# Cross-attention and a LoRA mixture-of-experts layer on one core: the read-outs and scores of a quad gathered in one place

## The chip, the core and the metric

The kernel runs on one core of a Trainium2 chip. The metric is the device time of one launch in microseconds (us); the median of three runs of the kernel before is 1106.21 us (1106.09 to 1106.55). The engines are named as the profile names them: PE (TensorE matmul), PEld (TensorE weight load), DVE (VectorE), ACT (ScalarE), POOL (GpSimd) and SP (SyncE, which issues all DMAs here).

## The reference

The input x has 8 batches of 1024 rows of 1024 numbers; each batch has 64 memory rows and a mask over them. Everything is float32.

```python
h = layernorm(x)                                     # no weights
attn = softmax(where(mask, h @ memory.T / 32, -1e30))
x = x + where(any(mask), attn @ memory, 0)           # attention over 64 memory rows
h = layernorm(x)
base = h @ weight.T                                  # 1024 x 1024
probs = softmax(h @ router_w.T)                      # 8 experts
w = top-2 of probs, normalised, as a dense [rows, 8]
low = h @ lora_A.T                                   # 8 experts x rank 16 = 128 columns
out = x + base + 2 * ((low weighted by w) @ lora_B)
```

## The kernel before

**Tiles.** The 8192 rows are 64 tiles of 128 rows. Two tiles are a *pair* (0 to 31), four pairs are one batch, and two pairs are a *quad*. `quad(u)` works for u = 2, 4, ..., 30; the pairs 0 and 1 are done in `first()`. Inside a quad, u and v = u+1 are the pairs whose feed-forward part is computed. The pairs n = u+2 and m = u+3 have their attention finished in the same quad, and f = u+4 (and in the changed kernel g = u+5) have theirs begun. A quad is *far* while f exists (u up to 26).

**Order.** All five engine queues are written by hand (`tc.manual_schedule`): the order of the calls in `quad` is the order of each engine's instructions, and every engine works through its own queue in that order. What an instruction waits for is set by the tiles that it reads, and by the buffers that it takes over.

**Feed-forward.** The product h @ weight.T of a pair is done by a Strassen-Winograd scheme of seven block products. Product 1 is done for each pair alone (`product(u, 1)`, tile `ch`, 4 matmuls of 128x512); `product(u, 8)` adds the low-rank part to the same bank. Products 6, 2, 7, 3, 5 and 4 are done for both pairs of the quad by a second Strassen level (`joint(i, u, hooks)`, banks `jl` and `ju`, matmuls of 128x256, steps p4, chain, p2, p5, chain, p5, chain). `hooks[k]` are calls that are set between the steps. The sums of operands are POOL's (`rt_sums`, `rt_sum_3`, `joint_sums`, `six_add`), the additions of results into x are DVE's.

**Low rank and router.** `rt_turn_tile` turns the normalised rows (DVE transposes into hA and hB), `rt_low_rank_tile` multiplies them with 136 columns (tile `pa`), ACT copies the result (`axl`), `rt_top` makes the two weights on DVE, and `rt_turn_low_rank` turns it for the low-rank product (PE `trw`, ACT `axwt`).

**Attention of a pair.** `att_turn` turns x (DVE, `xs` into `xT`, two transposes of 128x1024). `att_scores` makes the scores with 16 matmuls of 64 columns, the two tiles in two halves of the array (`sct`). `att_sc` turns them back (`sc`), `att_rstd`, `att_shift`, `att_exp` and `att_divide` are the softmax on DVE and ACT, `att_turn_p` turns the weights (`ptp`, copied by ACT to `pt`). `att_readout` multiplies them with the memory in 4 matmuls of 64 rows and 512 columns into 4 banks (`ro`), and `att_add` adds the banks to x on DVE. The row statistics of x are ACT's (`x_sums`, `x_squares`, `x_root` for attention, `f_sums`, `f_squares`, `f_std` for the feed-forward, `f_rows` for the normalised rows, which go to DRAM and back as `hs`).

**What shares room.** One PSUM bank serves `sct`, `sc` and `ptp` in turn (`ps_at`), one serves `pa` and `trw` (`ps_rt`), and six serve all the rest (`ps_pp`: `ch` of both pairs, `ro`, `jl`, `ju`). A pool called `ring` has five tiles of 4 KB a partition, for `xs`, `xT`, `h`, `hs` and the blocked memory `ms`.

**The stretch that the change is about** runs from product 1 of u to the start of joint product 6 (the *head* of the quad). Before, PE does there, for u from 4 to 26: product 1 of u, `pa` of u, read-out of n, scores of m, `trw` of u, product 1 of v, product 8 of u, `pa` of v, read-out of m, scores of f. Every second quad (u = 4, 8, ..., 24) f begins a new batch, and then the memory of that batch is turned and centred in the head too (`load_ms`, `turn_mem`, `centre_turned` with the matmul `means`).

Of the kernel before, what the change touches and what calls it, by code (L numbers as in the profile page):

```python
# [10 lines left out]
F32 = mybir.dt.float32  # L11
# [13 lines left out]
def kernel(  # L25
# [61 lines left out]
    def transpose_blocked(dst, src):  # L87

        nc.vector.transpose(  # L89
            dst.rearrange("p k (t i) -> p t k i", i=NB),  # L90
            src.rearrange("p t (k i) -> p t k i", i=NB),
        )

    xts, xss, mems = {}, {}, {}

    def load_xs(u: int):

        xss[u] = []
        for r in range(2):
            xs = ring.tile([P, 4, QD], F32, tag="ring", name=f"xs_{u}_{r}")  # L100
            load_blocked(xs, xf[(2 * u + r) * P : (2 * u + r + 1) * P, :])
            xss[u].append(xs)

    def load_xt(u: int):
        xts[u] = []
# [237 lines left out]
    def load_ms(b: int):  # L343

        msr = ring.tile([P, D], F32, tag="ring", name=f"ms_{b}")
        n = M // NB * QD
        ms = msr[:, :n].rearrange("p (t c) -> p t c", c=QD)
        load_blocked(ms, mem[b])
        ones = msr[:, n : n + P]
        nc.gpsimd.memset(ones, 1.0 / D)  # L350
        mcs[b] = ms, ones, msr[:, n + P : n + P + M], msr

    def turn_mem(b: int):

        mt = memp.tile([P, KD, M], F32, tag="memT", name=f"memT_{b}_True", bufs=1)
        ms, ones, of_k, msr = mcs[b]
        transpose_blocked(mt, ms)
        if b == 1:
            nc.vector.tensor_reduce(of_k, mt.rearrange("p k m -> p m k"), AX.X, ALU.add)
        else:  # L360
            by = nc.gpsimd.tensor_tensor
            s4 = msr[:, : 4 * M].rearrange("p (k m) -> p k m", m=M)
            by(s4, mt[:, :4], mt[:, 4:], ALU.add)
            by(s4[:, :2], s4[:, :2], s4[:, 2:], ALU.add)
            by(of_k, s4[:, 0], s4[:, 1], ALU.add)
        mem_ts[b, True] = mt

    def centre_turned(b: int):

        _, ones, of_k, _ = mcs.pop(b)  # L370
        mt = mem_ts[b, True]
        means = bank_of(f"means_{b}")[:, :M]
        mm(means, ones, of_k, start=True, stop=True)
        tt(mt, mt, means.unsqueeze(1).to_broadcast([P, KD, M]), ALU.subtract)
# [16 lines left out]
    def xT_tile(u: int, r: int):  # L391
        t = ring.tile([P, KD, P], F32, tag="ring", name=f"xT_{u}_{r}")
        x_ts.setdefault(u, []).append(t)
        return t

    def att_turn_pe(u: int, r: int, later: bool = False):
        t = xT_tile(u, r)
        return transpose_pe((t[:, :KH, :], t[:, KH:, :]), xts[u][r], f"x{u}_{r}", later)

    def att_turn(u: int):  # L400
        for r in range(2):
            transpose_blocked(xT_tile(u, r), xss[u][r])

    def att_scores(u: int):

        mt = mem_ts[u // PPB, u > 1]
        sct = ps_at.tile([2 * M, P], F32, tag="at", name=f"sct_{u}")
        for k in range(KD):
            for r in range(2):
                mm(  # L410
                    sct[r * M : (r + 1) * M, :], mt[:, k, :], x_ts[u][r][:, k, :],
                    start=(k == 0), stop=(k == KD - 1),
                )
        scs[u] = small.tile([2 * M, P], F32, tag="tp", name=f"scts_{u}", bufs=2)
        nc.scalar.copy(scs[u], sct)
# [39 lines left out]
        tt(s, s, rden.unsqueeze(2).to_broadcast([P, 2, M]), ALU.mult)  # L455
        ps[u] = s

    def att_turn_p(u: int):
        ptp = ps_at.tile([2 * M, P], F32, tag="at", name=f"ptp_{u}")
        nc.tensor.transpose(ptp, ps.pop(u).rearrange("p j m -> p (j m)"), ident)  # L460
        pts[u] = small.tile([2 * M, P], F32, tag="tp", name=f"pt_{u}", bufs=2)
        nc.scalar.copy(pts[u], ptp)

    def att_readout(u: int):
# [13 lines left out]
    def att_add(u: int):  # L478
        for r in range(2):
            att_add_tile(u, r)  # L480
# [124 lines left out]
    def rt_turn_low_rank(u: int):  # L605
        axl = axls.pop(u)
        trw = ps_rt.tile([ER, 2, P], F32, tag="rt", name=f"trw_{u}")
        for r in range(2):
            nc.tensor.transpose(trw[:, r, :], axl[:, r, :ER], ident)  # L609
        axwts[u] = small.tile([ER, 2, P], F32, tag="axwt", name=f"axwt_{u}", bufs=2)  # L610
        nc.scalar.copy(axwts[u], trw)
# [66 lines left out]
    def add(u: int, bank, r: int, c: int):  # L678
        xc = xts[u][r][:, ts(c, HB)]
        tt(xc, bank, xc, ALU.add)  # L680
# [42 lines left out]
    def one_add(u: int):  # L723

        for to in ((0, 0), (0, 1), (1, 0)):
            add(u, pps[u][1], *to)

    def t_of(u: int):

# [43 lines left out]
        by(s3, up[:, :HK], lo[:, :HK], ALU.subtract)  # L773
        jss[i] = s1, s2, s3, s4

    def joint(i: int, u: int, hooks, final: bool = False):

# [15 lines left out]
        def to_x(p, src, first: int, n: int):  # L793
            if i == 6:
                t = t_of(p)[:, first : first + n]
                if n == HH and (p == u and first == 0 or v == NP - 1):
# [282 lines left out]

    def quad(u: int):  # L1080

        v, n, m, f = [u + i for i in range(1, 5)]
        more = n < NP
        far = f < NP
        b = f // PPB
        new_mem = far and f % PPB == 0

        product(u, 1, (lambda: att_sc(n)) if u == 2 else None, 1)
        if more and u > 2:
            x_sums(m)  # L1090
        if new_mem:
            mask_bias(b)
        pending.pop()()
        if u == 2:
            att_divide(n)
        one_add(u)
        rt_low_rank_tile(u, 0)
        if u == 2:
            att_turn_p(n)
        rt_low_rank_tile(u, 1)  # L1100
        if u == 2:
            att_turn(m)
        rt_turn_tile(v, 0)
        rt_top(u)
        rt_turn_tile(v, 1)
        rt_sum_3(u)
        rt_sums(v)
        if more and u > 2:
            x_squares(m)
        if new_mem:  # L1110
            load_ms(b)
        if far:
            load_xs(f)
            load_xt(f)
        if more:
            att_readout(n)
            att_scores(m)
            if u > 2:
                rt_turn_low_rank(u)
                x_root(m)  # L1120
                att_add(n)

        low_u = {3: lambda: rt_turn_low_rank(u)}
        if more:
            low_u = {0: lambda: att_sc(m), 2: lambda: product(u, 8)}
            if u == 2:
                low_u[1] = lambda: rt_turn_low_rank(u)
        product(v, 1, low_u)
        if more:
            att_rstd(m)  # L1130
            att_exp(m)
            if u == 2:
                att_add(n)
                att_divide(m)
        else:
            product(u, 8)
        product_add(u, 8)
        if more:
            f_sums(n)
            if u > 2:  # L1140
                att_divide(m)
        if new_mem:
            turn_mem(b)
        one_add(v)
        rt_low_rank_tile(v, 0)
        if more:
            att_turn_p(m)
        rt_low_rank_tile(v, 1, (lambda: centre_turned(b)) if new_mem else None)
        joint_sums(6, u)
        rt_sum_3(v)  # L1150
        if far:
            att_turn(f)
        rt_top(v)
        if more:
            f_squares(n)
            f_std(n)
            att_readout(m)
        if far:
            att_scores(f)
        if new_mem:  # L1160
            load_mem(b)
        if more:
            att_add(m)

        hooks = {7: [lambda: rt_turn_low_rank(v)]}
        if more:
            row_0, row_1 = f_rows_steps(n)
            hooks = {2: [row_0], 5: [lambda: rt_turn_low_rank(v), row_1]}
        end_6 = joint(6, u, hooks)
        joint_sums(2, u)  # L1170

        def low_v():
# [5 lines left out]
            for p in (u, v):  # L1178
                six_add(p)

        hooks = {1: [six]}
        if far:
            x_stats(f)
            hooks[3] = [lambda: att_sc(f)]
        if new_mem:
            void_mem(b)
        if (f + 2) % PPB == 0 and f + 2 < NP:
# [19 lines left out]
            hooks[5].append(lambda: att_exp(f))  # L1207
        end_3 = joint(3, u, hooks)
        joint_sums(5, u)
        if m + 2 < NP:  # L1210
            load_xs(m + 2)

        hooks = {1: [end_3]}
        if far:
# [8 lines left out]
        def rows_0():  # L1223
            end_5()
            for p in (u, v):
                store(p, 0)
                if not more:
                    store(p, 1, ts(1, HB))
            if m + 2 < NP:
                load_xt(m + 2)  # L1230

        hooks = {1: [rows_0]}
        if more:
            hooks[3] = [lambda: rt_sums(n)]
        if m + 2 < NP:
            hooks[5] = [lambda: att_turn(m + 2)]
        end_4 = joint(4, u, hooks, not more)

        def last():
# [56 lines left out]
```

## Time and profile before

| what | value |
|---|---|
| median of 3 runs | 1106.21 us (1106.09 to 1106.55) |
| the profiled execution, its time | 1106.56 us |
| its span, first to last instruction | 1104.7 us |
| PE busy | 1095.7 us (99%) |
| DVE busy | 810.8 us (73%) |
| POOL busy | 575.9 us (52%) |
| ACT busy | 555.3 us (50%) |
| granted TensorE clock | 1.000 |
| HBM traffic | 172.85 MB, 156 GB/s over the span |

A float32 matmul is two records in the trace, so that 16 matmuls are shown as x32. Matmuls overlap: how long one really takes is the distance from its start to the next one's start, not the length of its record. All times in the text are distances of starts where a row is followed by another on the same engine.

### The profile page before, as it was taken

How to read it: one execution, taken by the hardware profiler on the slowest of the kernel's cores; microseconds unless marked ns; L12 is line 12 of the kernel's file. 1: busy time of each engine (PE TensorE's matmuls, PEld its weight loads, DVE VectorE, ACT ScalarE, POOL GpSimd, SP SyncE). 2: the span in 40 equal slices, each digit the busy share in tenths (PEclk: the TensorE clock that was granted, in tenths of full speed). 3: DMA queues.
4: the chain of work that ended last, by engine and by line, in shares of the span. 5: the costliest groups of instructions: out<-in, count | busy, mean ns of one | idle time of the engine just before them, and what ended most of it. 6: DMA issues, size and time to landing. Idle time of an engine off the chain costs nothing.

```text
span 1104.7 us, 17542 instructions
## 1 busy us (share of the span) xinstructions
PE 1095.7 (99%) x5864; PEld 848.1 (77%) x5864; DVE 810.8 (73%) x2063; ACT 555.3 (50%) x1063; POOL 575.9 (52%) x647
## 2 busy tenths in 40 slices
PE   8999999999999999999999999999999999999998
PEld 6554787887878778787887878778787887878877
DVE  6666968777786768867678686777868787686665
ACT  4577554718357282663727547173562826545010
POOL 0079564735637265473635647266372744637382
PEclk9999999999999999999999999999999999999999
DMA  9857356374554735456265553754446453532301
GB/s 230 210 177 222 113 166 201 100 238 132 154 182 136 222 109 183 151 164 218 77 211 162 154 190 101 215 166 157 153 139 203 145 190 132 158 131 91 138 1 77
DMA packets 104922, 174.01 MB, mean 158 GB/s; under 512 B 12929, under 2 KB 77441, under 8 KB 104833
## 3 DMA queue, kind: packets, MB, share of 16 engines
q1 hardware_dynamic: 104832, 172.90, 50.3%
q8 instruction: 47, 0.77, 0.3%
q14 instruction: 43, 0.34, 0.1%
HBM read 107.84 MB, written 65.01 MB: 156 GB/s over the span
## 4 chain that ended last, share of the span: by engine, by line
PE 98%; DVE 1%; ACT 0%; DMA 0%; issue 0%; SPq 0%; DVEq 0%; ACTq 0%
PE jl L691 28%; PE ju L691 21%; PE pa L569 11%; PE ch L691 10%; PE sct L410 6%; PE ro L471 5%; PE ju L683 4%; PE jl L683 3%; PE plain L691 3%; PE ch L683 2%; PE j L691 1%; PE trw L609 1%; DMA xt<-in_x_dram 0%; PE tr_x L385 0%; PE b L691 0%; PE ptp L460 0%
## 5 line engine op out<-in xcount | busy, mean ns | idle before, releaser
L805 DVE TENSOR_TENSOR xt<-jl,xt 128x256 f32<-128x256 f32 x421 | 191.3, 484 | 115.8 <-PE jl L691 75.6
L805 DVE TENSOR_TENSOR xt<-ju,xt 128x256 f32<-128x256 f32 (+1 forms) x210 | 110.6, 550 | 69.9 <-PE ju L691 67.3
L623 POOL TENSOR_TENSOR s<-hA,hB 128x512 f32<-128x512 f32 x31 | 39.6, 1278 | 208.8 <-PE jl L691 92.8
L195 ACT ACTIVATE junk<-xt 128x1024 uint8<-128x1024 f32 x60 | 63.2, 1053 | 138.2 <-DMA xt<-in_x_dram 137.7
L735 POOL TENSOR_TENSOR xt<-xt,hA 128x512 f32<-128x512 f32 x90 | 111.3, 1275 | 23.5 <-DVE hA L801 23.4
L691 PE MATMUL ch<-w,hA 128*128 128x512 f32 x248 | 115.8, 593 | 0.0
L630 POOL TENSOR_TENSOR hA<-hA 128x512 f32<-128x512 f32 x31 | 39.4, 1272 | 141.3 <-PE pa L569 141.3
L691 PE MATMUL ju<-w,s_j 128*128 128x256 f32 x360 | 94.3, 384 | 0.2
L691 PE MATMUL ju<-t,s_j 128*128 128x256 f32 x360 | 92.5, 379 | 0.0
L680 DVE TENSOR_TENSOR xt<-ch,xt 128x512 f32<-128x512 f32 x124 | 79.4, 680 | 8.4 <-PE ch L691 4.5
L680 DVE TENSOR_TENSOR xt<-ro,xt 128x512 f32<-128x512 f32 x128 | 79.2, 676 | 3.3 <-PE ro L471 3.3
L691 PEld LDWEIGHTS ju<-t,s_j 128*128 128x128 f32 x360 | 66.2, 190 | 16.3 <-issue 3.6
L691 PEld LDWEIGHTS ch<-w,hA 128*128 128x128 f32 x248 | 44.6, 190 | 42.7 <-issue 41.8
L691 PEld LDWEIGHTS ju<-w,s_j 128*128 128x128 f32 x360 | 63.9, 190 | 16.4 <-issue 7.4
L691 PE MATMUL jl<-t,s 128*128 128x256 f32 x300 | 76.0, 384 | 0.0
L569 PEld LDWEIGHTS pa<-art_sb,hA 128*128 128x128 f32 x512 | 66.3, 190 | 9.0 <-issue 5.0
L89 DVE STREAM_TRANSPOSE xT<-xs 128x1024 f32<-128x1024 f32 x60 | 72.6, 1228 | 0.5
L410 PEld LDWEIGHTS sct<-xT,memT_True 128*64 128x64 f32 x960 | 53.1, 137 | 24.8 <-issue 12.1
L569 PE MATMUL pa<-art_sb,hB 128*128 128x136 f32 x512 | 71.1, 280 | 0.0
L569 PE MATMUL pa<-art_sb,hA 128*128 128x136 f32 x512 | 69.9, 279 | 0.0
L204 ACT ACTIVATE junk<-xt,of_x 128x1024 uint8<-128x1024 f32 x60 | 68.7, 1145 | 1.5
L253 ACT ACTIVATE junk<-xt,of_f 128x1024 uint8<-128x1024 f32 x60 | 68.7, 1145 | 1.5
(205 smaller groups left out, 2448.6 us busy)
## 6 DMA issues: line engine op xcount, KB each, us to landing
xt<-in_x_dram SPq DMA_DIRECT2D x64, 512.0 KB, 4.6
out_dram<-xt SPq DMA_DIRECT2D x62, 512.0 KB, 2.7
xs<-in_x_dram SPq DMA_DIRECT2D x240, 128.0 KB, 3.6
hd<-h SPq DMA_DIRECT2D x60, 512.0 KB, 2.7
hs<-hd SPq DMA_DIRECT2D x240, 128.0 KB, 3.2
mem<-in_ctx_dram SPq DMA_DIRECT2D x16, 256.0 KB, 3.8
w<-in_w_t_dram SPq DMA_DIRECT2D x16, 256.0 KB, 10.2
ms<-in_ctx_dram SPq DMA_DIRECT2D x28, 64.0 KB, 2.5
```

The lines of the kernel that those rows point to most:

```text
L89: nc.vector.transpose(dst.rearrange("p k (t i) -> p t k i", i=NB), src.rearrange("p t (k i) -> p t k i", i=NB),)
L195: nc.scalar.activation(nowhere, xts[u][r], AF.Identity, accum_out=sm[:, r, :])
L204: nc.scalar.activation(nowhere, xts[u][r], AF.Square, bias=nm[:, r, :], accum_out=ss[:, r, :],)
L253: nc.scalar.activation(nowhere, xts[u][r], AF.Square, bias=nm[:, r, :], accum_out=ss[:, r, :])
L410: mm(sct[r * M : (r + 1) * M, :], mt[:, k, :], x_ts[u][r][:, k, :], start=(k == 0), stop=(k == KD - 1),)
L471: mm(ro, pts[u][rows, :], m[rows, ts(c, HB)], start=True, stop=True)
L569: mm(pa[:, r, :], h, art_sb[:, k, :], start=(k == 0), stop=(k == KD - 1))
L680: tt(xc, bank, xc, ALU.add)
L683: mm(bank, axwts[u][:, r, :], lb_sb[:, c0 : c0 + n], start=alone, stop=True, skip_group_check=True)
L691: mm(bank, a[:, k, :], w[:, k, :], start=(start and k == 0), stop=(k == n - 1), skip_group_check=True)
L735: nc.gpsimd.tensor_tensor(xc, xc, t_of(u), ALU.add)
L805: tt(xc, src, xc, ALU.add)
```

## The change

- **One cluster in the head.** For u from 4 to 26 the read-out of n, the scores of f, the scores of g and the read-out of m now follow each other on PE, behind `pa` of both pairs and product 8 of u.
- **Scores of the second pair earlier.** The scores of g = u+5 are made in quad u, where before they were made in quad u+2. They take a bank of `ps_pp`, since `ps_at` is held by the scores of f. Quad 2 makes the scores of three pairs, quad 28 of none.
- **Turning of x.** Both f and g are turned by DVE in the head: four transposes there in place of two, and none in joint product 4, where the second pair was turned. Three of the four `xs` tiles are loaded in joint product 4, the fourth (`load_xs(g, (1,))`) when `hs` of v has been turned and has left its place in `ring`.
- **Order within the head.** Product 1 of v comes directly behind `pa` of u; `x_squares` of m is moved ahead of the copy `axl`; the low-rank turn of u gets a bank of `ps_pp` between the two tiles of `pa` of v; the softmax of m follows the top-2 of u; the weights of m are written back in place.
- **New memory.** It is loaded a quad earlier and turned in joint product 6 and centred in joint product 2. The sum over its 8 blocks is one DVE reduction in place of three POOL additions.
- **Row steps of n** (`f_squares`, `f_std`, `f_rows`) move into joint products 6 and 2. The three additions of product 1 of v are spread (`one_add(v, ...)`).

The core of the diff:

```diff
+        next_mem = f + 2 < NP and (f + 2) % PPB == 0
+        early = more and u == 2
+        late = more and u > 2
...
+        if late:
+            x_root(m)
+            product(v, 1, lambda: att_sc(m))
+            att_rstd(m)
+            att_shift(m)
+            att_exp(m)
         rt_turn_tile(v, 1)
+        if late and far:
+            att_turn_tile(f, 0)
+            load_xs(g, (1,))
         rt_sum_3(u)
         rt_sums(v)
...
+        if late:
+            att_divide(m)
+            if far:
+                att_turn_tile(f, 1)
+            rt_low_rank_tile(v, 0)
+            rt_turn_low_rank(u, bank_of(f"trw_{u}")[:, : 2 * P])
+            one_add(v, (0,))
...
+        if far:
+            for r in range(2):
+                att_turn_tile(g, r)
...
+        rt_low_rank_tile(v, 1)
+        if late:
+            att_turn_p(m, True)
+            product(u, 8)
         joint_sums(6, u)
         rt_sum_3(v)
+        if late and far:
+            att_readout(n)
         if more:
-            f_squares(n)
-            f_std(n)
-            att_readout(m)
+            product_add(u, 8)
+        if late and far:
+            att_add(n)
         if far:
             att_scores(f)
+            att_scores(g, True)
+        if next_mem:
+            load_ms((f + 2) // PPB)
+        if far or not more:
+            rt_top(v)
+        if more:
+            att_readout(m)
...
+        if late:
+            f_sums(n)
         if new_mem:
             load_mem(b)
...
+        elif more:
+            att_add(m)
...
+            hooks[2] = [lambda: f_squares(n), lambda: f_std(n)]
+        if next_mem:
+            hooks[5].append(lambda: turn_mem((f + 2) // PPB))
...
+            hooks[3].append(lambda: f_rows(n))
+        hooks[5] = []
+        if next_mem:
+            hooks[5].append(lambda: centre_turned((f + 2) // PPB))
...
-        if m + 2 < NP:
-            load_xs(m + 2)
...
-            if m + 2 < NP:
-                load_xt(m + 2)
+            if far:
+                load_xt(g)
+            if f + 2 < NP:
+                load_xs(f + 2)
+                load_xs(g + 2, (0,))
...
-        if m + 2 < NP:
-            hooks[5] = [lambda: att_turn(m + 2)]
```

In `turn_mem` the reduction on DVE, which only batch 1 used, is now used by all batches:

```diff
-        if b == 1:
-            nc.vector.tensor_reduce(of_k, mt.rearrange("p k m -> p m k"), AX.X, ALU.add)
-        else:
...
+        nc.vector.tensor_reduce(of_k, mt.rearrange("p k m -> p m k"), AX.X, ALU.add)
```

More of the change, by code (lines that the diff above doesn't have):

```diff
@@ L94, with load_xs @@
     xts, xss, mems = {}, {}, {}
-    def load_xs(u: int):
-        xss[u] = []
-        for r in range(2):
+    def load_xs(u: int, tiles=(0, 1)):
+        for r in tiles:
             xs = ring.tile([P, 4, QD], F32, tag="ring", name=f"xs_{u}_{r}")
             load_blocked(xs, xf[(2 * u + r) * P : (2 * u + r + 1) * P, :])
-            xss[u].append(xs)
+            xss.setdefault(u, []).append(xs)
     def load_xt(u: int):
@@ L350, in load_ms @@
         nc.gpsimd.memset(ones, 1.0 / D)
-        mcs[b] = ms, ones, msr[:, n + P : n + P + M], msr
+        mcs[b] = ms, ones, msr[:, n + P : n + P + M]
     def turn_mem(b: int):
         mt = memp.tile([P, KD, M], F32, tag="memT", name=f"memT_{b}_True", bufs=1)
-        ms, ones, of_k, msr = mcs[b]
+        ms, ones, of_k = mcs[b]
         transpose_blocked(mt, ms)
-        if b == 1:
-            nc.vector.tensor_reduce(of_k, mt.rearrange("p k m -> p m k"), AX.X, ALU.add)
-        else:
[L361 to L365, printed above, removed]
+        nc.vector.tensor_reduce(of_k, mt.rearrange("p k m -> p m k"), AX.X, ALU.add)
         mem_ts[b, True] = mt
     def centre_turned(b: int):
-        _, ones, of_k, _ = mcs.pop(b)
+        _, ones, of_k = mcs.pop(b)
         mt = mem_ts[b, True]
@@ L398, in att_turn_pe, with att_turn_tile, att_scores @@
         return transpose_pe((t[:, :KH, :], t[:, KH:, :]), xts[u][r], f"x{u}_{r}", later)
+    def att_turn_tile(u: int, r: int):
+        transpose_blocked(xT_tile(u, r), xss[u][r])
     def att_turn(u: int):
         for r in range(2):
-            transpose_blocked(xT_tile(u, r), xss[u][r])
-    def att_scores(u: int):
+            att_turn_tile(u, r)
+    def att_scores(u: int, apart: bool = False):
         mt = mem_ts[u // PPB, u > 1]
-        sct = ps_at.tile([2 * M, P], F32, tag="at", name=f"sct_{u}")
+        if apart:
+            sct = bank_of(f"sct_{u}")[:, :P]
+        else:
+            sct = ps_at.tile([2 * M, P], F32, tag="at", name=f"sct_{u}")
         for k in range(KD):
@@ L456, in att_divide, with att_turn_p @@
         ps[u] = s
-    def att_turn_p(u: int):
+    def att_turn_p(u: int, in_place: bool = False):
         ptp = ps_at.tile([2 * M, P], F32, tag="at", name=f"ptp_{u}")
-        nc.tensor.transpose(ptp, ps.pop(u).rearrange("p j m -> p (j m)"), ident)
-        pts[u] = small.tile([2 * M, P], F32, tag="tp", name=f"pt_{u}", bufs=2)
+        s = ps.pop(u).rearrange("p j m -> p (j m)")
+        nc.tensor.transpose(ptp, s, ident)
+        if in_place:
+            pts[u] = s
+        else:
+            pts[u] = small.tile([2 * M, P], F32, tag="tp", name=f"pt_{u}", bufs=2)
         nc.scalar.copy(pts[u], ptp)
@@ L603, in rt_top, with rt_turn_low_rank @@
             tt(ax_e, ax_e, we[:, r, :].unsqueeze(2).to_broadcast([P, E, R]), ALU.mult)
-    def rt_turn_low_rank(u: int):
+    def rt_turn_low_rank(u: int, bank=None):
         axl = axls.pop(u)
-        trw = ps_rt.tile([ER, 2, P], F32, tag="rt", name=f"trw_{u}")
+        if bank is None:
+            trw = ps_rt.tile([ER, 2, P], F32, tag="rt", name=f"trw_{u}")
+        else:
+            trw = bank.rearrange("p (r i) -> p r i", i=P)
         for r in range(2):
@@ L721, in product_add, with one_add @@
                 add(u, chain, *to)
-    def one_add(u: int):
-        for to in ((0, 0), (0, 1), (1, 0)):
-            add(u, pps[u][1], *to)
+    def one_add(u: int, which=(0, 1, 2)):
+        for i in which:
+            add(u, pps[u][1], *((0, 0), (0, 1), (1, 0))[i])
     def t_of(u: int):
@@ L774, in joint_sums, with joint @@
         jss[i] = s1, s2, s3, s4
-    def joint(i: int, u: int, hooks, final: bool = False):
+    def joint(i: int, u: int, hooks, final: bool = False, aside: bool = False):
         v = u + 1
@@ L795, in to_x @@
                 t = t_of(p)[:, first : first + n]
-                if n == HH and (p == u and first == 0 or v == NP - 1):
+                if n == HH and (p == u and first == 0 or aside):
                     nc.scalar.copy(t, src)
@@ L1080, in quad @@
     def quad(u: int):
-        v, n, m, f = [u + i for i in range(1, 5)]
+        v, n, m, f, g = [u + i for i in range(1, 6)]
         more = n < NP
@@ L1086, in quad @@
         new_mem = far and f % PPB == 0
-        product(u, 1, (lambda: att_sc(n)) if u == 2 else None, 1)
-        if more and u > 2:
+        next_mem = f + 2 < NP and (f + 2) % PPB == 0
+        early = more and u == 2
+        late = more and u > 2
+        product(u, 1, (lambda: att_sc(n)) if early else None, 1)
+        if late:
             x_sums(m)
+            x_squares(m)
         if new_mem:
@@ L1093, in quad @@
         pending.pop()()
-        if u == 2:
+        if early:
             att_divide(n)
@@ L1097, in quad @@
         rt_low_rank_tile(u, 0)
-        if u == 2:
+        if early:
             att_turn_p(n)
         rt_low_rank_tile(u, 1)
-        if u == 2:
+        if early:
             att_turn(m)
@@ L1104, in quad @@
         rt_top(u)
+        if late:
[4 more added lines that the diff above has]
+            att_exp(m)
         rt_turn_tile(v, 1)
+        if late and far:
+            att_turn_tile(f, 0)
+            load_xs(g, (1,))
         rt_sum_3(u)
         rt_sums(v)
[L1108 to L1112, printed above, removed]
+        if early:
             load_xs(f)
+        elif far:
@@ L1114, in quad @@
             load_xt(f)
-        if more:
+        if late:
[5 more added lines that the diff above has]
+            one_add(v, (0,))
+        elif early:
             att_readout(n)
             att_scores(m)
[L1118 to L1129, printed above, removed]
+            load_xs(g, (0,))
+            product(
+                v, 1,
+                {0: lambda: att_sc(m), 1: lambda: rt_turn_low_rank(u), 2: lambda: product(u, 8)},
+            )
             att_rstd(m)
             att_exp(m)
-            if u == 2:
-                att_add(n)
-                att_divide(m)
+            att_add(n)
@@ L1135, in quad @@
+            att_divide(m)
+            f_sums(n)
+            att_turn_tile(f, 0)
+            load_xs(g, (1,))
+            load_xt(f)
+            rt_low_rank_tile(v, 0)
+            att_turn_p(m, True)
+            att_turn_tile(f, 1)
         else:
+            product(v, 1, {3: lambda: rt_turn_low_rank(u)})
             product(u, 8)
[L1137 to L1148, printed above, removed]
+            product_add(u, 8)
+            rt_low_rank_tile(v, 0)
+        if far:
+            for r in range(2):
+                att_turn_tile(g, r)
+        if late and not far:
+            att_readout(n)
+            att_add(n)
+        rt_low_rank_tile(v, 1)
+        if late:
+            att_turn_p(m, True)
+            product(u, 8)
@@ L1149, in quad @@
         joint_sums(6, u)
         rt_sum_3(v)
-        if far:
-            att_turn(f)
-        rt_top(v)
+        if late and far:
+            att_readout(n)
         if more:
-            f_squares(n)
-            f_std(n)
-            att_readout(m)
+            product_add(u, 8)
+        if late and far:
+            att_add(n)
         if far:
             att_scores(f)
+            att_scores(g, True)
[3 more added lines that the diff above has]
+            rt_top(v)
@@ L1160, in quad @@
+        if more:
+            att_readout(m)
+        if late and not far:
+            att_add_tile(m, 0)
+            rt_top(v)
+        if late:
+            f_sums(n)
         if new_mem:
             load_mem(b)
-        if more:
[L1163 to L1169, printed above, removed]
+        if late and not far:
+            att_add_tile(m, 1)
+        elif more:
+            att_add(m)
@@ L1170, in quad @@
+        left_over = []
+        if late:
+            one_add(v, (1,))
+            left_over.append(lambda: one_add(v, (2,)))
+        else:
+            one_add(v)
+        hooks = {5: left_over, 7: []}
+        hooks[5 if more else 7].append(lambda: rt_turn_low_rank(v))
+        if more:
+            hooks[2] = [lambda: f_squares(n), lambda: f_std(n)]
+        if next_mem:
+            hooks[5].append(lambda: turn_mem((f + 2) // PPB))
+        end_6 = joint(6, u, hooks, aside=not more)
         joint_sums(2, u)
@@ L1179, in six @@
                 six_add(p)
-        hooks = {1: [six]}
+        hooks = {1: [six], 3: []}
         if far:
             x_stats(f)
-            hooks[3] = [lambda: att_sc(f)]
+            hooks[3].append(lambda: att_sc(f))
+        if more:
+            hooks[3].append(lambda: f_rows(n))
+        hooks[5] = []
+        if next_mem:
+            hooks[5].append(lambda: centre_turned((f + 2) // PPB))
         if new_mem:
```

## Prediction

> **What bounds the kernel now.** I read the page's chain first, then PE's timeline of one quad, then DVE's for the same stretch.
>
> ```profile
> PE 98%; DVE 1%; ACT 0%; DMA 0%; issue 0%; SPq 0%; DVEq 0%; ACTq 0%
> ```
>
> PE carries 98% of the chain, and the list of waits gives PE about 5 us in all. PE's matmuls are the same before and after (same counts and shapes), so the change can win only what PE loses between them, and lose whatever it makes PE wait. PE's timeline of quad 10 shows the two clusters of the head:
>
> ```profile
> 380.72 1.09 PE L569 MATMUL pa<-art_sb,hB 128*128 128x136 f32 x8
> 381.74 1.99 PE L471 MATMUL ro<-mem,pt 64*128 64x512 f32 x8
> 383.66 1.97 PE L410 MATMUL sct<-xT,memT_True 128*64 128x128 f32 x32
> 385.56 0.44 PE L609 MATMUL trw<-ident,axl 128*128 128x128 f32 x2
> 385.83 1.02 PE L691 MATMUL ch<-w,hA 128*128 128x512 f32 x2
> ...
> 393.13 1.09 PE L569 MATMUL pa<-art_sb,hB 128*128 128x136 f32 x8
> 394.15 1.99 PE L471 MATMUL ro<-mem,pt 64*128 64x512 f32 x8
> 396.06 1.97 PE L410 MATMUL sct<-xT,memT_True 128*64 128x128 f32 x32
> 397.96 1.99 PE L691 MATMUL jl<-t,s 128*128 128x256 f32 x8
> 399.79 1.03 PE L691 MATMUL ju<-t,s 128*128 128x256 f32 x4
> ```
>
> Times are from start to start. The last group of `pa` takes 1.02 where the group before it takes 0.93 (379.79 to 380.72). The read-out takes 1.92, while its 8 records two abreast need 4 x 0.43 = 1.72 (0.43 is product 1's 3.44 through 8 records). The scores take 1.90 for 16 x 0.11 = 1.76, `trw` 0.27 for 0.22, `jl` 1.83 for 8 x 0.216 = 1.73. So each change of the array's shape costs 0.10 at the border, and 0.10 (512 or 256 columns) or 0.05 (128 columns) just behind it. The same timeline of quad 8, where the batch is new:
>
> ```profile
> 327.05 1.99 PE L471 MATMUL ro<-mem,pt 64*128 64x512 f32 x8
> 328.97 2.42 PE L410 MATMUL sct<-xT,memT_True 128*64 128x128 f32 x32
> 331.32 1.99 PE L691 MATMUL jl<-t,s 128*128 128x256 f32 x8
> ```
>
> Here the scores take 2.35, 0.45 more than 1.90: they wait for the new turned memory. DVE in the head of quad 10:
>
> ```profile
> 382.26 0.24 DVE L582 MAX8 top<-axl 128x8 f32<-128x8 f32 x2 [0.43 <-ACT axl L574]
> 384.82 0.70 DVE L89 STREAM_TRANSPOSE hA<-hs 128x512 f32<-128x512 f32 x1
> 386.04 2.44 DVE L680 TENSOR_TENSOR xt<-ro,xt 128x512 f32<-128x512 f32 x4
> 388.41 0.14 DVE L420 RECIPROCAL of_x<-of_x 128x2 f32<-128x2 f32 x1
> ...
> 392.72 2.35 DVE L89 STREAM_TRANSPOSE xT<-xs 128x1024 f32<-128x1024 f32 x2
> 395.00 0.19 DVE L582 MAX8 top<-axl 128x8 f32<-128x8 f32 x2
> 397.51 2.47 DVE L680 TENSOR_TENSOR xt<-ro,xt 128x512 f32<-128x512 f32 x4
> 399.91 0.15 DVE L277 RECIPROCAL of_f<-of_f 128x2 f32<-128x2 f32 x1
> ```
>
> From 382.26 on DVE has hardly a gap. It is no bound over the span (73%), but in the head it is nearly as full as PE, and the change adds two turns there.
>
> **Gain 1, fewer changes of shape.** Cluster one costs (0.10+0.10) into the read-out, (0.10+0.05) into the scores, (0.10+0.05) into `trw`: 0.50. Cluster two ends in `jl` and costs 0.55. The new cluster is read-out, scores, scores, read-out, `jl`: 0.20 + 0.15 + 0 + 0.20 + 0.20 = 0.75. Saved: 0.30 in each of the 12 quads from 4 to 26, 3.6; quad 28 saves one change (0.1), quad 2 none.
>
> The Trainium skill, TensorEngine Tiling (Array Packing), Key Properties, says that changing the tiling mode, not just the tile, drains the engine; it gives no price. The Trainium skill, TensorE: Matmul & The Clock Gate, Single matmul latency, has a fixed part of about 166 ns for a warm matmul that stands alone; one per change saved is an estimate of 25 x 0.166 = 4.2 where the rows give 3.7.
>
> **Gain 2, new memory.** Six quads (4, 8, ..., 24) lose the 0.45 above, and 0.08 in `jl` of product 6 (0.94 for 0.86 in quad 8's rows, where DVE comes late behind the memory's steps). The matmul `means` costs 0.22 where it stands and 0.22 where it goes. Saved: 6 x 0.53 = 3.2. What hides the moved steps: in product 6 DVE idles 1.54 and 1.52 between its copies, and gets the turn of 0.70 and the reduction, 1.07 in the one place where the trace has it. That makes `six_add` on POOL about 0.75 late. POOL's first sum for product 7 is done at 413.75 and PE uses it at 414.80, 1.05 later, so I book nothing; with that cover gone it is 0.3 x 6 = 1.8. POOL's three additions (1.5 us) go: nothing waits for them afterwards.
>
> **The cost: DVE's row in the head.** Zero is the start of product 1 of u (374.07). PE's new order with the rows above: `pa` of u ends at 7.57, product 1 of v with `sc` at 11.12, `pa`, `trw`, `pa` of v at 15.04, `ptp` and product 8 at 16.01; the read-out of n begins at 16.1, scores of f 18.0, scores of g 19.8, read-out of m 21.7, joint 6 at 23.6 (23.9 before).
>
> DVE begins its top-2 of u at 8.19, as before. Then, in its new order: top-2 2.56 (382.26 to 384.82); start of the softmax of m 1.05 (388.41 to 389.45); second turn of v 1.22, to 13.0; turn of f 1.14 (half of 392.72 to 395.00); division 0.63, to 14.8; turn of f 1.14; one addition 0.60; turns of g 1.14 each, to 18.8; addition of product 8 0.60, to 19.4; four additions of n 2.37, to 21.8; top-2 of v 2.51, to 24.3; the first addition of m is over at 25.0.
>
> Who waits for it: `ptp` at 15.04 (weights ready 14.8); scores of g at 19.8 for the bank that product 8 leaves (19.4, about 0.1 for the record's end and the signal); the read-out of m at 21.7 and 22.1 for the banks of n (the last at 21.8); joint 6's upper bank at 23.6 + 1.8 = 25.4 (25.0). So DVE holds with 0.2 to 0.4 to spare, if nothing in its queue waits.
>
> One thing in it does: the fourth `xs` tile is issued by SP only when the second turn of v has left its place in `ring`, at 13.0. Four DMAs about 0.47 apart put the last at 14.5. The page gives for such a DMA:
>
> ```profile
> xs<-in_x_dram SPq DMA_DIRECT2D x240, 128.0 KB, 3.6
> ```
>
> With 3.6 to landing it is there at 18.1, DVE wants it at 17.7. Behind the waiting turn stand the addition of product 8 and those of n, and behind these on PE the scores of g and the read-out of m. Bounds: 2.5 to landing (`ms`, 64 KB) costs nothing; 4.6 (`xt`, 512 KB) makes DVE 1.4 late, 1.1 more than it has to spare. I take 3.6, its own row: 0.4 late, 0.2 of it PE's, 12 x 0.2 = 2.4 (0 to 13).
>
> The Trainium skill, TensorEngine Tiling (Array Packing), PSUM Bottleneck, speaks against the cluster: tiling speeds up PE but not the emptying of PSUM. By that rule the cluster, not its borders, would set the time. The rows of this case: eight banks are 8 x 0.59 = 4.7 of DVE, plus 2.5 for the top-2 between them, against 7.5 of PE from 16.1 to 23.6, so emptying does not bind unless DVE comes late to it.
>
> **ACT** keeps its 64 table loads. `axwt` of v now stands behind `f_squares` and `f_std` of n: sums from 22.5 to 25.0, copy to 25.8, squares 2.5, table load and root 1.6, `axwt` done at 30.3; PE wants it 7.2 after joint 6 begins, at 30.8. In quad 28 there are no scores, joint 6 begins earlier and that cover is gone: 0.5 (0 to 1). `x_squares` ahead of `axl` fits before 7.8 where the second tile of x has landed by 3.8; in quads 10 and 12 it landed at 4.2, and the head is 0.4 late there.
>
> **Quad 2.** After the division (123.5) DVE makes four turns (4.6) and product 8's addition before scores that PE could begin at 127.6: 1.1 lost; the 0.57 that its scores lose now (127.73 to 130.20) goes: 0.6 net (0 to 2.5). The load queues of SP move the same bytes; `xs` loads sit ahead of the second stores, whose places are wanted 8 us later: nothing.
>
> **Sum.** -3.6 - 0.1 - 3.2 + 2.4 + 0.5 + 0.6 = -3.4. The profiled execution took 1106.56 (span 1104.7), 0.35 above the median of 1106.21: 1103.2 in its terms, 1102.8 as a median.
>
> **Rivals.**
> - *All hidden* (0.15): the fourth tile lands by 17.6. For it: the queue is empty then, and only four DMAs go. Against it: 3.6 is a median over many such. Then -6.9 + 0.6: 1099.3 to 1101.
> - *Eaten up* (0.25): DVE is 0.5 late at each border, through L455 (0.29 to 0.89 in the rows) or a turn at 1.22 as in joint 4. 12 x 0.5 = 6.0 against 2.4: 1106.4; the case covers 1104 to 1108.4.
> - *Slower* (0.15): the fourth tile lands late. Place: DVE's fourth turn, in each of 12 quads. Every 0.1 beyond the spare is 1.2 us. It turns the sign when PE waits 0.48 a quad in place of 0.2, and goes over +0.2% from 0.67, at about 4.1 to landing; at 4.6 it is 1113.
> - The forecast itself (0.45): 1101 to 1104.
>
> What this kernel can tell from no change is about 0.2%, 2.2 us, so faster means under 1104.0 and slower over 1108.4. Faster 0.15 + 0.45 = 0.60, same 0.25, slower 0.15. The range leaves a tenth out on each side: 1099.6 (all hidden) to 1109.0 (a little into slower).
>
> **What would show it.** Right: one border into and out of the cluster in PE's timeline, scores of f and g 3.6 together; no wait for `memT`; DVE's fourth turn of x idle under 0.6 before it on a DMA; joint 6 23.6 to 24.0 after product 1. Wrong: an idle DVE of over 0.8 before that turn, scores of g over 2.2, or PE waiting in joint 6 and 2 for `hA` or `axwt` in ordinary quads.

## The result, and the profile after

| kernel | median, us | lowest to highest | ratio to before, 95% interval |
|---|---|---|---|
| before | 1106.22 (8 runs) | 1106.09 to 1106.86 | 1 |
| changed | 1108.53 (8 runs) | 1106.87 to 1111.37 | 1.0023 [1.0014, 1.0032] |

The forecast was 1102.8: the change is slower by 0.23%, where a gain of 0.3% was expected. The spread differs too: the kernel before stays within 0.8 us, the changed one moves over 4.5. Its profiled execution took 1107.39 (span 1105.5), 1.1 under its median; all sums over its trace below are 1.1 smaller than what the median run pays.

The chain of waits of the changed kernel, shares by engine:

```profile
PE 87%; DMA 6%; DVE 4%; ACT 2%; issue 0%; SPq 0%; DVEq 0%; ACTq 0%
```

Before, PE had 98% of it. PE is as full as before by its busy time (99%), but the chain now leaves it for transfers, DVE and ACT. The list of waits (total us, times, longest) says which:

```profile
ACT junk L194 <- DMA xt<-in_x_dram: 156.6, 26, 9.8
...
DVE top L587 <- ACT axl L579: 21.1, 16, 3.5
...
PE pa L574 <- DVE hA L89: 1.4, 4, 0.5
...
PE ptp L462 <- DVE s L456: 1.2, 2, 1.0
...
PE jl L699 <- ACT hA L806: 0.7, 1, 0.7
...
PE ju L699 <- DVE hA L808: 0.5, 1, 0.5
...
DVE xT L89 <- DMA xs<-in_x_dram: 0.3, 1, 0.3
```

The first two were 137.7 and 12.5 before. `DVE xT <- DMA xs`, the wait on which the forecast put its cost, has 0.3 in all. PE's own waits add up to little here, because a late matmul is often drawn as a long one before it; they are read from starts. PE's timeline of quad 10, the cluster:

```profile
391.12 1.99 PE L476 MATMUL ro<-mem,pt 64*128 64x512 f32 x8
393.04 3.71 PE L411 MATMUL sct<-xT,memT_True 128*64 128x128 f32 x64
396.68 1.99 PE L476 MATMUL ro<-mem,s 64*128 64x512 f32 x8
398.60 1.78 PE L699 MATMUL jl<-t,s 128*128 128x256 f32 x7
```

The cluster does what was forecast: both scores in 3.64 without a border and without a wait for `memT` or for DVE; product 6 begins 23.59 after the quad's start at 375.01, forecast 23.6. The head of quad 12, a little ahead of the cluster, does not:

```profile
454.46 0.38 PE L617 MATMUL trw<-ident,axl 128*128 128x128 f32 x2
455.37 1.19 PE L574 MATMUL pa<-art_sb,hA 128*128 128x136 f32 x8 [0.52 <-DVE hA L89]
456.40 1.09 PE L574 MATMUL pa<-art_sb,hB 128*128 128x136 f32 x8
457.56 0.30 PE L462 MATMUL ptp<-ident,s 128*128 128x128 f32 x1
```

`trw` takes 0.22 where nothing waits; here the second tile of `pa` of v starts 0.91 after it, 0.69 late, and `ptp` 1.16 after the last group, where 0.93 is usual. ACT in the same quad, which starts at 441.50 (changed kernel, the reading of accumulators left out):

```profile
442.48 1.06 ACT L194 ACTIVATE junk<-xt 128x1024 uint8<-128x1024 f32 x1 [9.78 <-DMA xt<-in_x_dram]
...
446.86 1.06 ACT L194 ACTIVATE junk<-xt 128x1024 uint8<-128x1024 f32 x1 [3.23 <-DMA xt<-in_x_dram]
...
448.27 1.15 ACT L203 ACTIVATE junk<-xt,of_x 128x1024 uint8<-128x1024 f32 x1
...
449.55 1.15 ACT L203 ACTIVATE junk<-xt,of_x 128x1024 uint8<-128x1024 f32 x1
...
450.70 0.36 ACT L579 COPY axl<-pa 128x272 f32<-128x272 f32 x1
```

And before, where the quad starts at 440.64:

```profile
444.79 1.06 ACT L195 ACTIVATE junk<-xt 128x1024 uint8<-128x1024 f32 x1 [2.64 <-DMA xt<-in_x_dram]
...
448.41 0.39 ACT L574 COPY axl<-pa 128x272 f32<-128x272 f32 x1 [2.23 <-PE pa L569]
...
449.40 1.13 ACT L204 ACTIVATE junk<-xt,of_x 128x1024 uint8<-128x1024 f32 x1
```

Before, ACT had summed x_m and sat idle for 2.23 until `pa` of u was there; the squares came behind `axl`. Now sums, mean and both squares stand ahead of `axl`: 3.84 from the landing of the second tile of x_m to `axl`. The tile landed at 5.36 after the quad's start (here and below a landing of x_m is read as ACT's start on the tile, in the rows that waited about 0.1 behind the last part of the transfer), `axl` started at 9.20 in place of 7.77, and DVE's row with the top-2 of u, the softmax of m and the second turn of v started that much later. The quads, by these readings (us after the quad's start; the period is start to start):

| changed kernel | second tile of x_m | `axl` of u | second tile of `pa` of v | `ptp` | period |
|---|---|---|---|---|---|
| quad 26 | 2.10 | 7.77 | 13.19 | 15.04 | 66.26 |
| quad 4 | 3.91 | 7.77 | 13.19 | 15.04 | 66.26 |
| quad 6 (memory turned) | 4.36 | 8.20 | 13.19 | 15.06 | 66.53 |
| quad 24 | 4.77 | 8.61 | 13.29 | 15.48 | 66.72 |
| quad 20 | 5.15 | 8.99 | 13.66 | 15.85 | 67.09 |
| quad 12 | 5.36 | 9.20 | 13.87 | 16.06 | 67.31 |

An `axl` at 8.20 costs PE nothing to speak of (quad 6); what it is later than that, PE pays nearly in full.

Before, the tile landed at 2.05 to 3.23 in 11 of 13 quads and at 4.15 and 4.21 in two; now at 3.9 to 5.4 in 11 of 13 (not in quad 28, where no `xs` follows it, and not in quad 26, where it does, for a reason that no run shows). What lies beside it in the DMA engines, 440 to 450 us, the head of quad 12 in the changed kernel (packets, then the issues with KB and median time to landing):

```profile
DMA packets 1619, 2.25 MB, mean 225 GB/s; under 512 B 172, under 2 KB 1370, under 8 KB 1618
...
xs<-in_x_dram SPq DMA_DIRECT2D x12, 128.0 KB, 7.0
xt<-in_x_dram SPq DMA_DIRECT2D x1, 512.0 KB, 7.0
```

The same bytes as in the kernel before in that stretch (2.19 MB), but 1370 packets under 2 KB for 509: the 12 `xs` DMAs right behind x_m move 1 KB packets.

### The profile page after: what moved, and what is told of

Read it like the earlier page. It is cut to its first block, busy times and chain, and to the rows that moved or that the text cites. A ratio compares the mean times of both kernels' runs of the same rounds, so it can differ in the third digit from the quotient of the medians.

```text
span 1105.5 us, 17565 instructions
## 1 busy us (share of the span) xinstructions
PE 1093.1 (99%) x5864; PEld 846.3 (77%) x5864; DVE 816.9 (74%) x2069; ACT 557.5 (50%) x1063; POOL 567.8 (51%) x629
## 4 chain that ended last, share of the span: by engine, by line
PE 87%; DMA 6%; DVE 4%; ACT 2%; issue 0%; SPq 0%; DVEq 0%; ACTq 0%
PE jl L699 26%; PE ju L699 20%; PE pa L574 8%; PE ch L699 7%; PE ro L476 6%; PE sct L411 5%; PE ju L691 3%; PE jl L691 3%; DMA xt<-in_x_dram 3%; PE plain L699 3%; PE ch L691 2%; DMA out_dram<-xt 1%; DVE xt L814 1%; ACT junk L203 1%; PE j L699 1%; DMA w<-in_w_t_dram 1%
## 5 line engine op out<-in xcount | busy, mean ns | idle before, releaser
L295 ACT ACTIVATE h<-xt,of_f 128x1024 f32<-128x1024 f32 x60 | 71.2, 1232 | 23.6 <-DVE of_f L291 17.4
L699 PEld LDWEIGHTS ju<-t,s_j 128*128 128x128 f32 x360 | 66.1, 190 | 17.4 <-issue 5.0
```

The lines of the kernel that those rows point to most:

```text
L295: nc.scalar.activation(h, xts[u][r], AF.Identity, bias=nmr[:, r, :], scale=rstd[:, r, :])
L699: mm(bank, a[:, k, :], w[:, k, :], start=(start and k == 0), stop=(k == n - 1), skip_group_check=True)
```

## The experiments

Each ran beside the kernel before on one chip. The kernel before had medians of 1106.0 to 1106.3 there, so medians of different experiments can be compared to some 0.3. Two theories stood against each other: that x_m lands late and ACT passes it on, and that DVE's row with the fourth `xs` tile is the cost, as the prediction had it.

**1. x_m tile by tile on ACT.**

```diff
-            x_sums(m)
-            x_squares(m)
+            x_by_tile(m)     # sum, mean, squares of tile 0; then of tile 1
```

> ACT takes the two tiles of x_m one after the other (sum, mean, squares of the first, then of the second) in place of both sums and then both squares; nothing else differs from the changed kernel. Theory (the second tile of x_m lands at 3.8 to 5.4 after the quad's start, ACT still has 3.84 of work from that landing to the copy axl, and axl, the top-2, the second turn of v and PE come late for it): only about 2.7 is left behind the landing, axl is due before 8.2 in every quad, the waits of PE at the second tile of pa of v and at ptp go (5.5 in the profiled run, about 6.6 in the median run), 1101.5 to 1103. Rival 1 (DVE's row in the head is too long by itself, as the prediction had it, through the fourth xs tile): axl's time matters little, 1107 to 1109. Rival 2 (the landing is late by so much that only the transfer's start helps): half of the gain, 1105.

Measured: 1103.87 (1102.59 to 1105.40), ratio 0.9978 [0.9969, 0.9988], 0.9 above the expected range. `axl` is at 7.77 in 9 of the 12 quads from 4 to 26, though the tile still lands late (3.3 to 5.9 in 11 of them; in quad 22 it was there ahead of ACT). PE waits for `axl` in one quad alone, 0.28 in quad 20, where the tile landed at 5.87. So ACT's order in front of `axl`, together with the late landing, cost 4.7 of the median run. In quads 10 and 12 something else shows: the scores of g are late by 0.21 and 1.39.

**2. `xs` away from x_m.**

```diff
+        if f + 2 < NP:               # ahead of joint product 5
+            load_xs(f + 2)
...
-            if f + 2 < NP:           # behind load_xt(g) in joint product 4
-                load_xs(f + 2)
-                load_xs(g + 2, (0,))
...
         pending.pop()()
+        if late and far:
+            load_xs(g, (0,))
```

> The 12 DMAs of xs that SP issues right behind the two loads of x_m are moved: 8 (both tiles of f) to the place ahead of joint product 5 where the kernel before loads its xs, 4 (first tile of g) behind the second stores, 7 after the quad's start. ACT's order stays that of the changed kernel. Theory (these DMAs share the 16 DMA engines with the second tile of x_m and make its last parts land at 3.8 to 5.4 in place of 2.0 to 3.2): the second tile lands by 3.2 in nearly every quad, axl is at 7.8, 1101.5 to 1103. Rival (the landing is late by chance, as it was in quads 10 and 12 of the kernel before and was not in quad 26 of the changed one, and xs has no part in it): landing stays at 4 to 5, 1107 to 1109. Cost if g's first tile comes late: 0 to 0.5 a quad, at its turn.

Measured: 1103.40 (1102.05 to 1104.79), ratio 0.9972 [0.9961, 0.9983], 0.4 above the expected range. The tile lands at 1.94 to 3.14 in all 13 quads and `axl` is at 7.77 in all of them. ACT in quad 12 of this run, which starts at 508.57:

```profile
511.48 1.06 ACT L194 ACTIVATE junk<-xt 128x1024 uint8<-128x1024 f32 x1 [1.12 <-DMA xt<-in_x_dram]
...
516.34 0.39 ACT L579 COPY axl<-pa 128x272 f32<-128x272 f32 x1 [0.93 <-PE pa L574]
```

So the 12 DMAs behind x_m are what made it late. What is left over is in two quads; DVE and PE in quad 10 of this run (start 373.93):

```profile
393.73 1.25 DVE L89 STREAM_TRANSPOSE xT<-xs 128x1024 f32<-128x1024 f32 x1 [2.41 <-DMA xs<-in_x_dram]
394.89 0.65 DVE L688 TENSOR_TENSOR xt<-ch,xt 128x512 f32<-128x512 f32 x1
```

```profile
391.96 1.97 PE L411 MATMUL sct<-xT,memT_True 128*64 128x128 f32 x32
395.60 1.97 PE L411 MATMUL sct<-xT,memT_True 128*64 128x128 f32 x32 [1.67 <-DVE xt L688]
```

This is the wait that the prediction named, with the queue that it named: the fourth turn waits for its tile, behind it stands the addition of product 8, and the scores of g wait for its bank. But it comes in some quads only: the last part of that tile landed at 17.0 to 17.4 in ten quads, at 18.3 in one and 19.7 in this one; DVE wants it at 17.4.

**3. Only a third of the load behind x_m** (the 8 DMAs of f moved, the 4 of g left).

> As the run before, but the 4 DMAs of the first tile of g stay behind x_m: a third of the load. Theory: the second tile of x_m lands between 2 and 4, and less often late; 1101.5 to 1104. Rival (chance): 1107 to 1109.

Measured: 1110.54 (1106.63 to 1113.45), ratio 1.0036 [1.0025, 1.0048]: a miss. Four DMAs were enough to make the tile late, though less often (3.7 to 5.4 in 8 of 12 quads, where twelve had 3.9 to 5.4 in 11); `ptp` came 3.0 late in all for it, where the changed kernel has 5.2. What made this run slower is the fourth tile: its last part landed at 19.4 to 20.3 in quads 8, 10 and 12 (17.1 to 18.7 in the changed kernel's profile), and the scores of g waited 4.3 for product 8. Why it was so late here is not settled.

**4. Quad 28 alone.**

```diff
-        if late:
+        if late and far:
             f_sums(n)                  # in quad 28: hooks[2] of product 6
...
+            left_over.append(lambda: one_add(v, (1, 2)))      # quad 28
...
+            hooks[5] += [lambda: f_squares(n), lambda: f_std(n)]
```

> The changed kernel with quad 28 alone mended: f_sums of n behind the first copy of joint product 6 on ACT, f_squares and f_std behind axwt, and the second addition of product 1 of v later on DVE. Theory: in quad 28 PE's waits of 0.68 and 0.54 in joint product 6 go, 1.2 less, 1107.3 in the median. Rival (axwt or the rows of n come late instead): 1108 to 1109.

Measured: 1108.62 (1106.18 to 1110.75), ratio 1.0015 [1.0005, 1.0025]; the spread of the changed kernel hides it. By the trace quad 28 takes 63.77 for 64.42: the wait of 0.68 for ACT's copy is gone, that for DVE's copy is 0.81 where it was 0.54. Half of what was expected.

This trace shows more. Up to quad 26 the kernel is the changed one, and this execution (1109.95) is one of its longer ones: quads 4 to 26 lose 9.0. Of that 4.5 is there at `ptp`, behind `axl`; the other 4.5 comes behind it, most of it (3.4 in the list of waits) scores of g that wait for the addition of product 8, since the fourth tile landed at 20.7 in quad 8 and at 19.5 in quad 10. So a longer execution can pay for the fourth tile as much as for x_m, which the profiled execution of the changed kernel hides.

**5. The fourth tile early**, on top of experiment 2: it takes the place of the first tile of `hs` of v, the turned tile of f that of the second.

```diff
         rt_turn_tile(v, 0)
+        if late and far:
+            load_xs(g, (1,))
...
         rt_turn_tile(v, 1)
         if late and far:
             att_turn_tile(f, 0)
-            load_xs(g, (1,))
```

> The kernel with xs moved apart, and in it the fourth xs tile (second tile of g) takes the place in ring that the first turn of v leaves, 5 us earlier than the one that the second turn leaves; the turned tile of f takes the latter, on the engine that has just freed it. Theory (beside x_m there is the second cause, the one that the prediction named: in a few quads a part of the fourth tile lands at 18.3 to 19.7, and the scores of g wait for the addition of product 8 that stands behind its turn; 2.0 in the profiled run with xs apart): the DMAs of the tile are issued before 10, it lands before 14, these waits are gone in every quad, 1100.5 to 1102, and the spread of the runs (1102.05 to 1104.79) shrinks to under 1. Rival (the spread comes from elsewhere): 1103 to 1104 with the same spread.

Measured: 1101.92 (1101.83 to 1103.53), ratio 0.9965 [0.9951, 0.9978]. Every quad from 4 to 26 takes 66.26, or 66.48 where memory is turned; no wait of the scores is left. As expected but for one run of five, which lies 1.4 above the others.

**6. The fourth tile early, alone**, on the changed kernel.

> The changed kernel with one mend: the fourth xs tile takes the place that the first turn of v leaves. The other xs tiles stay behind x_m, ACT's order stays. Theory (two causes: the late x_m, some 4.7 by the run tile by tile, and the late fourth tile, 1.5 by the difference of the two runs with xs apart): 1106.5 to 1107.5, the waits for axl stay, those of the scores for the addition of product 8 are gone. Rival (the fourth tile was the main cause, as the prediction had it): 1102 to 1104.

Measured: 1107.17 (1104.85 to 1107.85), ratio 1.0007 [0.9998, 1.0016]; the waits of the scores are gone and those for `axl` stay. By the medians the fourth tile was worth 1.4 here and 1.5 between experiments 2 and 5, and x_m the larger part; the intervals of these runs overlap, so the size is rough.

**7. What makes the fourth tile late?** The loads of x of f go ahead of it, on top of experiment 2, so that nothing follows it.

> The kernel with xs apart, and the two 512 KB loads of x of f moved on SP from right behind the fourth xs tile to 5 us ahead of it; the fourth tile is issued as late as there, 13 to 15 after the quad's start, now with nothing behind it. It asks what makes the fourth tile's last part land late in some quads. Theory (a transfer is stretched by what is queued right behind it, as x_m is by xs): it lands by 17.3 in every quad, the scores of g wait nowhere, about 1102, the spread under 1 as with the fourth tile early (1101.83 to 1103.53). Rival (a part is late by itself, whatever follows): 1103 to 1104 with waits of 1 to 2 in one or two quads, as with xs apart (1102.05 to 1104.79).

Measured: 1103.28 (1102.26 to 1105.89), ratio 0.9973 [0.9964, 0.9982]. The theory falls: with nothing behind it the tile still landed at 18.2 in quads 8 and 10, which lost 0.39 and 0.56. What delays a part of it stays open.

**8. `x_squares` where the kernel before has it**, behind `axl`.

> The changed kernel with x_squares of m behind the copy axl and the scale of the top-2, where the kernel before has them. Theory: axl of u is at 7.77 and pa of v no longer waits, but squares, root and softmax of m come 2.4 later and ptp waits for its weights, which were ready 0.25 before they were wanted: 2 us in each of 13 quads, 26 less the 6 that the late axl cost: about 1128. Rival (the softmax has room): 1102 to 1104.

Measured: 1130.43 (1127.33 to 1133.49, at granted clocks of 0.995 to 0.999), ratio 1.0228 [1.0212, 1.0244]. `axl` is at 7.77 and `ptp` at 16.83 in place of 15.04, though the tile of x landed at up to 6.2; quads take 68.1 to 68.4, one 69.3. About as expected (1128): the softmax of m has no room in this head, and its squares can't simply stand behind `axl`.

**9. All mends together** (experiments 1, 2, 4 and 5).

> The mends together: x_m tile by tile on ACT, xs apart, the fourth tile early, and quad 28 with f_sums of n behind the first copy of product 6. Theory: every quad from 4 to 26 takes 66.26 (66.48 where new memory is turned), quad 28 takes 63.2 to 63.8, nothing in the head waits: span about 1097.5, 1099 to 1100.5 in the median, spread under 1. Rival (something else still waits): 1101 to 1103.

Measured: 1101.19 (1100.89 to 1101.90), ratio 0.9955 [0.9942, 0.9969]. It beats both kernels, and its runs lie within 1.0 again. Every quad is as expected (66.26 or 66.48, and 63.83 in quad 28). The median is 0.7 above the expected range; the quads are not the reason, I summed too low: 175.5 up to quad 4, 796.2 for the quads to 26, 63.8 for quad 28 and 64.2 to the end are the span of 1099.7.

**10. The scores of g behind the read-out of m**, in the mended kernel.

> The mended kernel with one change in PE's order: the scores of g behind the read-out of m, so that the cluster is read-out, scores, read-out, scores and has one change of shape more in each of 12 quads; DVE keeps its order. Theory (a change from read-out to scores or back costs 0.10 at the border and 0.05 to 0.10 behind it): quads of 66.46 to 66.6, 2.4 to 4 in all, plus up to 0.2 a quad where the scores wait for the last bank of n. Rival (the clusters gained by something else, and a border costs nothing): 66.26 as before.

Measured: 1118.72 (1118.41 to 1119.76), ratio 1.0116 [1.0101, 1.0131]: 67.73 a quad, far over what was expected. PE in quad 10 of this run:

```profile
396.14 1.97 PE L426 MATMUL sct<-xT,memT_True 128*64 128x128 f32 x32
398.04 2.45 PE L491 MATMUL ro<-mem,s 64*128 64x512 f32 x8
400.42 1.97 PE L426 MATMUL sct<-xT,memT_True 128*64 128x128 f32 x32
403.20 1.97 PE L714 MATMUL jl<-t,s 128*128 128x256 f32 x8 [0.82 <-DVE xt L703]
```

The two scores take 1.90 and 1.90 by their own work, where they took 3.64 together: 0.15 for the border. The rest of the 1.47 is banks: the read-out takes 2.38 for 1.92, and `jl` waits 0.82, for additions that DVE makes in its old order. I had put that at 0.2.

**11. The scores of f ahead of the read-out of n**, in the mended kernel: one border more, and no bank wanted earlier.

```diff
         if late and far:
+            att_scores(f)
             att_readout(n)
...
-            att_scores(f)
             att_scores(g, True)
```

> The mended kernel with the scores of f ahead of the read-out of n: scores, read-out, scores, read-out, so that the cluster has one change of shape more, while no bank is wanted earlier than DVE leaves it (the read-out of n is 1.9 later, DVE adds product 8 first in any case). Theory (the run with the scores of g behind the read-out of m paid 0.15 of its 1.47 a quad for the border and the rest for banks): quads of 66.41 for 66.26, 1.8 in all, 1103.0 in the median. Rival (borders cost 0.10 or less): under 1102.4; rival (the 1.47 was the border): 1118.

Measured: 1103.07 (1102.20 to 1103.65), ratio 0.9974 [0.9963, 0.9985]. Quads of 66.41 and 66.63, 0.15 more in each, and no wait beside: one border costs 0.15. The median is as expected to 0.1 us, though the runs spread over 1.45.

**12. The kernel before with its 8 `xs` DMAs behind x_m.**

> The kernel before, with its 8 DMAs of xs issued right behind the two loads of x_m in joint product 4 in place of ahead of joint product 5; nothing else. Theory (packets of 1 KB beside those of 4 KB make the last parts of x_m late): the second tile of x_m lands between 3 and 5.5 after the quad's start in most quads, where it lands at 2.0 to 3.2 (4.1 in two). The time says little: squares of m wait for axl there, and the turns of x in joint product 4 may now come late. Rival: 2.0 to 3.2 as before.

Measured: one run, 1210.32, granted clock 0.965. The second tile of x_m landed at 3.5 to 6.2 in 11 of 13 quads. SP issues it 1.9 ahead of the quad's start as before; from issue to the last part it takes 6.0 in the median of the 13 quads, where the kernel before has 4.6, the changed one 6.6 and experiment 2 again 4.5. So the order of the DMAs does it, without the rest of the change. The time is no measure of that: the turns of x in joint product 4 wait for their tiles there (105.8 in all).

## Why the prediction was wrong

By its own steps, on the trace of the changed kernel:

| step | forecast | measured in the profiled execution |
|---|---|---|
| fewer changes of shape, quads 4 to 26 | -3.6 | -3.6: 66.26 for 66.56 in quads where nothing waits, 0.30 x 12 |
| new memory | -3.2 | -3.2: such quads lose 0.76 (67.32 to 66.56), the quads that turn it now pay 0.22 |
| the fourth `xs` tile | +2.4 | +0.4: what is left of the 5.6 by which the periods from 4 to 26 (801.8) exceed 12 x 66.26 + 5 x 0.22 = 796.2 |
| x_m and `axl` | nothing | +5.2: `ptp` later than 15.04, all quads from 4 to 26 |
| quad 28 | +0.4 | +1.6: it gains 0.34, though 1.90 of scores left it |
| quad 2 | +0.6 | +0.4: quad 4 starts 2.50 later, of which 1.90 are scores of g and 0.22 `means` |
| sum | -3.4 | +0.8 (1107.39 against 1106.56) |

Both gains were right to a tenth, and so was the place of product 6 where nothing waits; experiment 11 bears out the price of a border. Three steps failed.

**The transfer behind which DMAs were put.** The working says of the load queues that they "move the same bytes" and books nothing for them, and it checks `x_squares` ahead of `axl` with the landing times of the kernel before: it "fits before 7.8 where the second tile of x has landed by 3.8". Both ends of this were in hand: 3.84 of ACT's work behind a landing, and a change that puts 12 DMAs right behind that transfer. The working even saw two quads, 10 and 12, in which "the head is 0.4 late", and no term of its sum holds them. But the landing was taken as fixed. Experiment 1 takes away ACT's part, experiment 2 the DMAs; each brings 4.7 to 5.1 of the median run back, and experiment 12 makes the landing late in the kernel before. The term was put at nothing, for a reason ("the same bytes") that the runs refute.

**The fourth tile.** Mechanism, place and queue were right, the size and the manner were not. The forecast took 3.6 to landing, the median of all `xs` DMAs, and a small wait in each of 12 quads. This tile takes 2.7 in an ordinary quad of experiment 2 (last DMA issued at 14.35, landed at 17.05): no wait in most quads, and 0.2 to 1.9 in a few where a part is late. It was worth some 1.4 of the median run (experiment 6), not 2.4, and up to 4.5 in one longer execution (experiment 4). That the sizes lie near the forecast is luck: it had a wait in each of 12 quads.

**Quad 28.** It was priced by `axwt` alone, 0.5. What came late were the copies of product 6: ACT's behind `f_sums` of n, 0.68, which experiment 4 takes away, and DVE's, 0.54, behind the top-2 of v in its queue, for which no run has a cure. The rest of the 1.6 is not traced.

The median lies 0.1 over the line between two rivals, and neither had its cause: "eaten up" (1104 to 1108.4) wanted DVE late by its own row, where the delay came through ACT, and "slower" wanted the fourth tile at 4.1 to landing in all 12 quads, which it took in a few. DVE's row, which the prediction thought nearly as full as PE, kept up in every quad where `axl` and the fourth tile were on time.

## What to carry to other kernels

When a change moves DMAs, ask what transfer they are put behind, and who waits for its last part; a landing time read from the old trace is not fixed. Work moved ahead of a copy in an engine's queue makes that copy wait for everything that the work waits for: count from the latest landing seen, and split the work by tiles so that only the late tile's share stands behind it. Look at the spread of the runs: here it was 4.5 us with two transfers ending on the path, under 1 in the kernel before and 1.0 with both taken off it, and the one execution that was profiled did not show what a longer one paid.

## What the hardware showed that was not expected

A transfer lands with its slowest part. In quad 8 of the changed kernel the 16 parts of the second tile of x_m were done at 1.5 to 1.9 (12 of them), 2.5 (two), and 4.7 and 4.8 after the quad's start. By the trace's packets, a 4 KB packet takes 159 ns (median, kernel before). In the changed kernel, from 2 us ahead of a quad's start to 7 behind it, the 282 that begin while eight or more 1 KB packets of `xs` are in flight take 264 (median); of the 186 that begin with one to seven in flight, four in five still take 159. That fits a late part being stretched further once the others have gone on to the next transfer; no run takes the two apart, nor does one move `xs` in larger packets.

The Trainium skill, DMA: Bandwidth & Descriptors, Why a DMA increments its semaphore by 16 and not by 1, has the same picture: a DMA's engines finish independently, and only the full count says that the data has landed. That agrees with the parts above. The same page, Why small descriptors are slow, gives a fixed overhead of about 3 cycles per packet; by that working a 1 KB packet would lose some 9% (an estimate). The traces have 46 ns for a 1 KB packet (median), 16% over a quarter of 159, and neither accounts for 264 in place of 159.

Why some parts are late at all, the fourth tile's too, the runs do not show.
